# Four layers of graph attention on one core: moved copies, and two groups of VectorE work tied to a place in its order

## The chip, the cores and the metric

The kernel runs on one NeuronCore of one Trainium2 chip. The metric is the device time of one execution in microseconds (us), and smaller is better. A core has TensorE (matmuls), VectorE, ScalarE, GpSimd (POOL) and SyncE (SP), which here only issues transfers. Each engine works through its own list of instructions in order. In profile lines the engines are called PE (its weight loads PEld), DVE, ACT, POOL and SP.

## The reference

Input x is 4096 rows of 256 floats, `adj` a symmetric 4096 x 4096 matrix of zeros and ones with a filled diagonal. Four attention layers follow each other; each adds its result to x and normalises the rows:

```python
x = _layernorm(x + _L0_gnn_ref(x, adj, L0_gnn_W, L0_gnn_a), axis=-1)
x = _layernorm(x + _L1_gnn_ref(x, adj, L1_gnn_Wq, L1_gnn_bq, L1_gnn_Wk, L1_gnn_bk, L1_gnn_Wv, L1_gnn_bv), axis=-1)
x = _layernorm(x + _L2_gnn_ref(x, adj, L2_gnn_W, L2_gnn_a), axis=-1)
x = _layernorm(x + _L3_gnn_ref(x, adj, L3_gnn_Wq, L3_gnn_Wk), axis=-1)
```

The first layer has four heads and additive scores: `e = leaky_relu(s_i + s_j)` with both terms from `h @ W`, masked by `adj`, a softmax over j, the weighted sum of `h @ W`, and an elu. The second has four heads with q, k and v from x, and exponentials of q.k where `adj` has an edge. The third is additive with one head. The fourth takes the cosine between projections of x, its exponential where there is an edge, and returns half of the weighted mean of x plus half of x:

```python
raw_att = Kn @ Qn.T
att = jax.nn.softmax(jnp.where(adj > 0, raw_att, NEG) * TEMP, axis=1)
prop_fea = att @ features
return (1.0 - KEEP_RATIO) * prop_fea + KEEP_RATIO * features
```

## The kernel before, in words

x lies in SBUF for the whole kernel, as tile X of 32 row tiles of 128. The result is made in 8 blocks (NB) of 512 columns (QW); for each block a loop runs over the 32 row tiles j (64 half tiles in the second layer). Such a pair (block, j) is a unit. In each unit ScalarE makes the raw weights, VectorE masks them by a slice of `adj`, and TensorE multiplies them with the features and sums over j in PSUM. TensorE's sums run LAG units behind the weights.

The order on each engine comes from a scheduler, which places instructions by its own idea of their times, except inside a `manual_schedule` block, where the named engines keep the program's order. In the first layer and in the opening of the second this is TensorE alone, in the last layer none until its ending. `tc.issue_after(i)` around an instruction forbids the scheduler to place it ahead of instruction i.

**Start of the first layer** (additive_heads). `turn(b)` transposes block b of x on TensorE (L117) and copies it out of PSUM into xT (L119); `busy` (L357) says on which engines, one copy for each half of the features. `prepare(b)` multiplies it by the weights (L215) into a PSUM tile `side` of three banks and one further bank, takes exponentials (L219 to L221) and stores the values V (L222). For block 0, `first_rows` (L267) lays the source terms of the four heads out as rows in four PSUM banks: one bank of its own for head 0, three of tile `over` for heads 1 to 3. It does so by four transposes a head (L272). `weights(0, 0)` reads these rows straight out of PSUM (L299), one activation a head, and then `keep_rows` (L275) copies them to SBUF, for odd heads on VectorE and for even ones on ScalarE (L277), for later units to read. The mask product is L302, the sums are L312. `first_rows`, `turn(1)`, unit 0, `turn(2)` and `prepare(1)` come in this order, then unit 1.

**Opening of the second layer** (multi_head_attention). Blocks 2 to 7 of x are transposed by `block_apart`: VectorE transposes 32 x 32 squares (L129, two instructions) into a tile of which one buffer exists, SP sends it to DRAM (`far<-squares`, L133) and fetches it back rearranged (`xT<-far`, four transfers, L137). For each block `keys` makes q and k (L755), ScalarE adds the bias (L763), VectorE takes the greatest absolute value of each (L764, into kbig and qbig). `values` makes v (L774) and VectorE stores it (L781). In turn b the program has block_apart(b + 1), values(b - 1), keys(b); the last turn has no values ahead of keys. Before them the first layer's tail for the last block runs (outputs, L324 to L331, add_elu, layernorm), and its `turn(1)` (L747) copies on ScalarE.

**Last layer** (cosine_attention). In each unit `scores` (L1138) and an exponential (L1142) are made; in every second unit `weights` masks two tiles at once (L1151) and `mix_weights` makes three differences (L443 to L445), with which seven products (L453) do the work of eight. After a block `outputs` puts the quarters together and `squares_far` transposes them by squares (L1172), sends them to DRAM (L1176) and fetches them back (L1179) into `kept2`. `outputs_far(b - 1)` is called at j = 10 of the lagging loop of the next block: it sums the fetched rows (L1186), scales and adds them to y (L1190), takes row statistics (one_row, L156 and L157), a root (Ln and Exp on ScalarE, L161 and L162) and stores the rows (L1203).

Of the kernel before, what the change touches and what calls it, by code (L numbers as in the profile page):

```python
# [18 lines left out]
P = 128  # L19
D = 256  # L20
# [8 lines left out]
def kernel(  # L29
# [205 lines left out]
    def additive_heads(a, H, slope, early, narrow, ahead):  # L235
# [7 lines left out]
        with ExitStack() as lay:  # L243
# [23 lines left out]
            def first_rows(banks):  # L267

                row[0] = rp.tile([P, H, QW], FP, name="row")
                for h in range(H):  # L270
                    for k in range(QB):
                        nc.tensor.transpose(banks[h][:, k * P:(k + 1) * P],  # L272
                                            src[:, k, h:h + 1].to_broadcast([P, P]), ident)

            def keep_rows(banks):  # L275
                for h in range(H):
                    (nc.vector.tensor_copy if h % 2 else nc.scalar.copy)(row[0][:, h, :], banks[h])  # L277

            def rows(b, pr):

# [10 lines left out]
            def weights(b, j, rows=None):  # L291
                m = b, j // MJ
                if j % MJ == 0:
                    mask[m] = mp.tile([P, MJ, QW], I32, name="mask")
                    nc.sync.dma_start(mask[m], edges[:, j:j + MJ, b * QW:(b + 1) * QW])
                z = prob[b, j] = zp.tile([P, H, QW], FP, name="prob")
                for h in range(H):
                    r = rows[h] if rows else row[b][:, h, :]
                    nc.scalar.activation(z[:, h, :], r, AF.Relu, bias=-1.0, scale=dst[:, j, h:h + 1])  # L299
                if rows:  # L300
                    keep_rows(rows)
                nc.vector.scalar_tensor_tensor(z, z, 1.0, mask[m][:, j % MJ, :].unsqueeze(1).to_broadcast([P, H, QW]),  # L302
                                               OP.add, OP.mult)

# [49 lines left out]
            def turn(b, bank=bank):  # L354
                if b + 2 < NB:
                    load_x(b + 2)
                busy = (nc.scalar.copy if b == 0 else nc.vector.tensor_copy,  # L357
                        nc.vector.tensor_copy if b == 1 else nc.scalar.copy)
                xTs[b] = transposed_block(sb, bank, b, busy)

            def prepare(b):
# [6 lines left out]
            with tc.manual_schedule(engines={mybir.EngineType.PE}):  # L368


                over = pa.tile([P, HC + 1, QW], FP, name="acc")
                side = pa.tile([P, HC + 1, QW], FP, name="acc")

                def warm(n):

                    for _ in range(n):
                        nc.tensor.matmul(over[:, 0, :P], ones, ones, start=True, stop=True)

                warm(2)
                nc.tensor.matmul(side[:, 0, :], ones[:1, :], a_row, start=True, stop=True)  # L380
                attach(keep, w_sb, side[:, 0, :], H)
                turn(0)
                warm(2)
                prepare(0)
                banks = [bank()] + [over[:, h, :] for h in range(H - 1)]
                first_rows(banks)
                free = iter([side[:, 0, :], side[:, 1, :]])
                turn(1, lambda: next(free))
                for i in range(len(units) + LAG):
                    if i < len(units):  # L390
                        b, j = units[i]
                        weights(b, j, None if i else banks)
                        if (b, j) == (1, 4 * QB):
                            early()
                        if i % 8 == 4:
                            narrow(prob[b, j][:, 0, :1])
                    if i >= LAG:
                        b, j = units[i - LAG]
                        sums(b, j)
                        if b:  # L400
                            finish(b - 1, j)

                    if i == 0 or i % QB == 3 and 3 + i // QB <= NB:
                        b = 1 if i == 0 else 2 + i // QB
                        if b + 1 < NB:
                            turn(b + 1)
                        prepare(b)
                        if b == 3:
                            rows(1, bank())
                    if i == (NB - 1) * NT + 20:  # L410
                        ahead(bank)
# [299 lines left out]
    def multi_head_attention(w_sb, b_sb, tail, rows_of_den, rows_done, narrow_edges, ga):  # L711
# [12 lines left out]
        with ExitStack() as lay:  # L724
# [7 lines left out]
            with ExitStack() as pro:  # L732
# [17 lines left out]
                def keys(b):  # L750
                    for n, to, scale in (("k", kT, 1.0), ("q", qT, qscale)):
                        for o in range(KC):
# [6 lines left out]
                            if n == "q" and b > 1:  # L759
# [1 line left out]
                                part, pk = (t.rearrange(how, a=QB, n=P // QB) for t, how in  # L761
                                            ((part, "p (k a n) -> p a k n"), (pk, "p (a k n) -> p a k n")))
                            nc.scalar.activation(part, pk, AF.Identity, bias=b_sb[n][:, o:o + 1], scale=scale)  # L763
                            nc.vector.tensor_reduce(big[n][:, b, o:o + 1], to[:, o, b * QW:(b + 1) * QW], AX.X, OP.max,  # L764
                                                    apply_absolute_value=True)

                def values(b):

# [35 lines left out]
                with tc.manual_schedule(engines={mybir.EngineType.PE}):  # L804
                    keys(0)
                    tail(bank, own)
                    turn(1)
                    for b in range(1, NB):
                        if b < NB - 1:
                            xTs[b + 1] = block_apart(sb, sq, dr, b + 1, nc.sync)  # L810
                        if b < NB - 1:
                            values(b - 1)
                        keys(b)
                        if b == 2:
                            ga.spread(bank, w2_sb)
                    values(NB - 2)
# [295 lines left out]
    def cosine_attention(co, tail):  # L1112
# [4 lines left out]
        with ExitStack() as lay:  # L1117
# [8 lines left out]
            pa = pool(lay, "co_pa", 1, space=PSUM)  # L1126
            ps = pool(lay, "co_ps", 2, space=PSUM)
            ov = out.rearrange("(t p) d -> p t d", p=P)
            mixed, acc, prob, mix, y, back = {}, {}, {}, {}, {}, {}

            def bank():
                return ps.tile([P, QW], FP, name="g")
# [11 lines left out]
            def weights(b, g):  # L1144
# [6 lines left out]
                nc.vector.tensor_tensor(z, z, co.mask[b, 2 * g // MJ][:, lo:lo + 2, :], OP.mult)  # L1151
                if b < NB - 1 or g < NP - LAST:
                    s = mix[b, g] = sb.tile([P, 4, HW], FP, name="mix")
                    mix_weights(s, z, nc.vector)

            def one_product(b, g, n):
                product(acc[b], prob[b, g], mix[b, g], mixed[g // 2][:, g % 2], g, n)
# [21 lines left out]
                nc.sync.dma_start(t, away.rearrange("r a m q s -> a r (m q s)"))  # L1179
                back[b, h] = t.rearrange("p (k f) -> p k f", k=2)  # L1180

            def outputs_far(b):
                mv = fin.tile([P, QB, 2], FP, name="mv")
                rden = fin.tile([P, QB], FP, name="rden4")
                for h in range(2):
                    nc.vector.tensor_reduce(rden[:, 2 * h:2 * h + 2], back[b, h], AX.X, OP.add)  # L1186
                nc.vector.tensor_scalar_mul(rden, rden, 2.0 / D)
                nc.vector.reciprocal(rden, rden)
                for k in range(QB):
                    nc.vector.scalar_tensor_tensor(y[b][:, k, :], back[b, k // 2][:, k % 2, :], rden[:, k:k + 1], y[b][:, k, :],  # L1190
                                                   OP.mult, OP.add)
                    one_row(mv, k, y[b][:, k, :])
                normalise([y[b][:, k, :] for k in range(QB)], mv)
                store(b, 0, QB, nc.sync)

            def rest(b, k, po, rden, mv):
                nc.vector.scalar_tensor_tensor(y[b][:, k, :], po, rden, y[b][:, k, :], OP.mult, OP.add)
# [88 lines left out]
                store(b, 3, 1, nc.sync)  # L1286

            units = [(b, j) for b in range(NB) for j in range(NT)]
            LAG = 4
            steps = {(0, j + n): (NB - 2 + b, step) for b, j in enumerate((1, 12)) for n, step in ((0, 3), (4, 3), (5, 1), (7, 2), (8, 3))}  # L1290
            for i in range(len(units) + LAG):
                if i < len(units):
                    b, j = units[i]
                    seen = scores(b, j)
                    if j % 2:
                        weights(b, j // 2)
                    if (b, j) == (0, 3):
                        tail(bank, cp)
                    if (b, j) == (0, 0):
# [4 lines left out]
                if i >= LAG:  # L1304
# [7 lines left out]
                    if i - LAG < len(units) - 2 * LAST:  # L1312
                        for n in range(7)[:4] if j % 2 == 0 else range(7)[4:]:
                            one_product(b, j // 2, n)
                        if j == NT - 1:
                            outputs(b)
                    if b and j == 10:
                        outputs_far(b - 1)
            with tc.manual_schedule(engines={mybir.EngineType.PE, mybir.EngineType.DVE, mybir.EngineType.Activation}):
                ending(NB - 1)  # L1320

# [89 lines left out]
```

## Time and profile before

| | us |
|---|---|
| Three runs | 2788.82, 2796.16, 2797.37 |
| Their median | 2796.16 |
| The profiled execution | 2794.14 |
| Its span, first to last instruction | 2792.4 |
| PE busy | 2772.5 |
| DVE busy | 2290.4 |
| ACT busy | 1702.9 |
| POOL busy | 1082.3 |
| The largest group, PE L312, 6144 records | 664.0 |

A group's line gives the kernel's line, the engine, the operation, the written tile, `<-`, the read tiles, and their sizes. In a list in order of time the first number is the start from the span's beginning and the second the stretch that `xN` such instructions took together. `[1.15 <-DVE prob L302]` says that the engine was idle for 1.15 us before it and that VectorE's instruction of line 302 ended this. In a list of waits the numbers are the total in us, how often, and the longest. A matmul of 32-bit floats leaves two records (a transpose one). Matmuls overlap and their ends are modelled, so the records' starts tell more than their ends.

### The profile page before, as it was taken

To read this page: it belongs to the slowest core of one execution; us is meant where nothing else is said; L and a number is where in the kernel's file an instruction comes from. 1 tells how busy PE (TensorE), PEld (TensorE's weight loads), DVE (VectorE), ACT (ScalarE), POOL (GpSimd) and SP (SyncE) were. 2 spreads that over 40 slices of the span, in tenths; PEclk is the share of its full clock that TensorE was granted. 3 is DMA by queue.
4 is the path that set the end of the run, shared out by engine and by line. 5 is a ranking of instruction groups with operands and counts; after the bars stand their busy time and mean duration, and the time that the engine had idled before them with its cause. 6 is when DMAs were issued, how large, how long until landed. Compare 5 with 4: busy or idle time off the path is not lost. (4 is left out here: it accounts for less than half of the span.)

```text
span 2792.4 us, 50485 instructions
## 1 busy us (share of the span) xinstructions
PE 2772.5 (99%) x19557; PEld 1449.7 (52%) x19557; DVE 2290.4 (82%) x3049; ACT 1702.9 (61%) x2668; POOL 1082.3 (39%) x1020
## 2 busy tenths in 40 slices
PE   9999999999999999999999999999999999999999
PEld 5333333333453333333333335888888777776776
DVE  8899999999677788887888878888888877776776
ACT  8899999999336666666666666465556422222222
POOL 0000100100029878778788787455455000000000
PEclk9999999999999999999999999999999999999999
DMA  7566676765339899998988988567778554444442
GB/s 207 107 142 137 138 144 130 136 143 114 69 97 193 184 178 196 192 188 184 195 182 189 190 182 187 174 199 213 181 207 238 109 82 76 77 72 78 72 74 43
DMA packets 275066, 411.94 MB, mean 148 GB/s; under 512 B 54809, under 2 KB 155657, under 8 KB 273930
## 3 DMA queue, kind: packets, MB, share of 16 engines
q0 software_dynamic: 104176, 182.74, 41.4%
q1 hardware_dynamic: 164280, 218.88, 26.2%
q10 hardware_dynamic: 6370, 7.10, 0.8%
q8 instruction: 153, 2.51, 0.4%
q14 instruction: 87, 0.71, 0.1%
HBM read 335.94 MB, written 39.40 MB: 134 GB/s over the span
## 5 line engine op out<-in xcount | busy, mean ns | idle before, releaser
L854 DVE TENSOR_TENSOR prob<-p,mask 128x1024 f32<-128x1024 f32 x512 | 619.7, 1222 | 165.9 <-ACT p L844 159.6
L844 ACT ACTIVATE p<-p,shift 128x1024 f32<-128x1024 f32 x512 | 555.7, 1088 | 319.4 <-PE p L842 319.2
L312 PE MATMUL acc<-prob,V 128*32 128x512 f32 x6144 | 664.0, 592 | 1.2 <-DVE prob L302 1.2
L299 ACT ACTIVATE prob<-row,dst 128x512 f32<-128x512 f32 x1020 | 635.1, 714 | 0.6
L302 DVE SCALAR_TENSOR_TENSOR prob<-prob,mask 128x2048 f32<-128x2048 f32 x256 | 580.4, 2286 | 25.7 <-ACT prob L299 25.0
L864 POOL TENSOR_TENSOR den<-den,prob 128x1024 f32<-128x1024 f32 x220 | 558.5, 2539 | 92.5 <-DVE prob L854 87.2
L842 PE MATMUL p<-qT,kT 64*64 64x512 f32 x4096 | 531.1, 590 | 2.2 <-DVE prob L854 2.2
L878 PE MATMUL acc<-prob,V 64*64 64x512 f32 x4096 | 529.9, 589 | 0.0
L312 PEld LDWEIGHTS acc<-prob,V 128*32 128x32 f32 x6144 | 197.3, 110 | 453.0 <-issue 432.2
L453 PE MATMUL acc<-mix,mixed 128*128 128x256 f32 x1476 | 402.1, 381 | 4.8 <-DVE mix L444 2.9
L453 PEld LDWEIGHTS acc<-mix,mixed 128*128 128x128 f32 x1476 | 278.7, 190 | 49.4 <-DVE mix L444 4.1
L878 PEld LDWEIGHTS acc<-prob,V 64*64 64x64 f32 x4096 | 157.4, 133 | 282.1 <-issue 280.3
L842 PEld LDWEIGHTS p<-qT,kT 64*64 64x64 f32 x4096 | 154.3, 133 | 279.2 <-issue 254.5
L90 POOL COPY tick<-prob 128x1 f32<-128x1 f32 x35 | 38.0, 1086 | 642.8 <-DVE prob L302 641.9
L1151 DVE TENSOR_TENSOR prob<-prob,mask 128x1024 f32<-128x1024 f32 x128 | 156.1, 1219 | 141.6 <-ACT prob L1142 141.6
L870 POOL DMA_DIRECT2D den<-prob x240 | 230.9, 962 | 61.2 <-DMA den<-prob 24.6
L1070 POOL DMA_DIRECT2D mask<-in_adjT x64 | 47.7, 745 | 532.6 <-DVE prob L1151 436.9
L453 PE MATMUL acc<-prob,X 128*128 128x256 f32 x984 | 252.6, 379 | 0.0
L453 PEld LDWEIGHTS acc<-prob,X 128*128 128x128 f32 x984 | 186.7, 190 | 78.8 <-issue 57.1
L586 DVE SCALAR_TENSOR_TENSOR prob<-r,own,mask 128x512 f32<-128x512 f32 x252 | 177.0, 743 | 49.0 <-POOL mix L445 13.0
L1142 ACT ACTIVATE prob<-p 128x512 f32<-128x512 f32 x144 | 86.0, 597 | 202.8 <-PE p L1138 202.8
L1142 ACT ACTIVATE prob<-g 128x512 f32<-128x512 f32 x112 | 66.9, 597 | 208.4 <-PE g L1138 208.4
(239 smaller groups left out, 2849.5 us busy)
## 6 DMA issues: line engine op xcount, KB each, us to landing
mask<-in_adjT SPq DMA_DIRECT2D x254, 512.0 KB
den<-prob POOLq DMA_DIRECT2D x240, 512.0 KB, 5.3
mask<-edges SPq DMA_DIRECT2D x512, 64.0 KB
mask<-in_adjT POOLq DMA_DIRECT2D x64, 512.0 KB, 5.7
edges<-in_adj POOLq DMA_DIRECT2D x32, 512.0 KB, 9.7
far<-squares SPq DMA_DIRECT2D x16, 512.0 KB
den<-prob SPq DMA_DIRECT2D x16, 512.0 KB
row<-far SPq DMA_DIRECT2D x7, 1024.0 KB
```

What stands on the lines that cost most here:

```text
L299: nc.scalar.activation(z[:, h, :], r, AF.Relu, bias=-1.0, scale=dst[:, j, h:h + 1])
L302: nc.vector.scalar_tensor_tensor(z, z, 1.0, mask[m][:, j % MJ, :].unsqueeze(1).to_broadcast([P, H, QW]), OP.add, OP.mult)
L312: nc.tensor.matmul(acc[b][h * G:(h + 1) * G, n, :], part, prob[b, j][:, h, :], start=(j == 0), stop=(j == NT - 1))
L453: nc.tensor.matmul(acc[at][:, half * HW:(half + 1) * HW], w, a, start=(g == 0 and n in (0, 2, 3, 5)), stop=(g == NP - 1), skip_group_check ...
L586: nc.vector.scalar_tensor_tensor(z[:, n, :], r, ga.own[:, j:j + 1], mask[:, n, :], OP.add, OP.mult)
L842: nc.tensor.matmul(p[c * d:(c + 1) * d, r, :], kT[half, c, at:at + d], qT[half, c, cols], start=True, stop=True)
L844: nc.scalar.activation(p, p, AF.Exp, bias=shift)
L854: nc.vector.tensor_tensor(z, p, mask[m][:, j % MJ, :].unsqueeze(1).to_broadcast([P, KC, QW]), OP.mult)
L864: nc.gpsimd.tensor_tensor(to, to, flat, OP.add)
L870: nc.gpsimd.dma_start(to, flat, accum_op=OP.add)
L878: nc.tensor.matmul(acc[b][c][r * d:(r + 1) * d, :], V[half, j, r * d:(r + 1) * d], prob[b, j][half, r, :], start=(j == 0), stop=(j == NH - 1))
L1151: nc.vector.tensor_tensor(z, z, co.mask[b, 2 * g // MJ][:, lo:lo + 2, :], OP.mult)
```

## The change

It has five pieces.

1. `first_rows` itself copies each head's row to SBUF, on VectorE, right after its four transposes; `keep_rows` is gone.
2. `turn(1)` copies both halves on ScalarE, where before VectorE copied both. `turn(2)` and later ones copy the first half on VectorE and the second on ScalarE, as before.
3. `prepare(1)` with its `turn(2)` comes after the weights of unit 1 instead of unit 0.
4. In the second layer's opening `keys` returns its last greatest-value instruction, and the next turn's `block_apart` may not be issued before it.
5. In the last layer `outputs_far` is cut into six steps, called at j = 15, 17, 19, 21, 23 and 25, each tied behind the last difference that `mix_weights` has made by then.

```diff
--- before.py
+++ after.py
@@ -271,10 +271,7 @@
                     for k in range(QB):
                         nc.tensor.transpose(banks[h][:, k * P:(k + 1) * P],
                                             src[:, k, h:h + 1].to_broadcast([P, P]), ident)
-
-            def keep_rows(banks):
-                for h in range(H):
-                    (nc.vector.tensor_copy if h % 2 else nc.scalar.copy)(row[0][:, h, :], banks[h])
+                    nc.vector.tensor_copy(row[0][:, h, :], banks[h])
 
             def rows(b, pr):
 
@@ -297,8 +294,6 @@
                 for h in range(H):
                     r = rows[h] if rows else row[b][:, h, :]
                     nc.scalar.activation(z[:, h, :], r, AF.Relu, bias=-1.0, scale=dst[:, j, h:h + 1])
-                if rows:
-                    keep_rows(rows)
                 nc.vector.scalar_tensor_tensor(z, z, 1.0, mask[m][:, j % MJ, :].unsqueeze(1).to_broadcast([P, H, QW]),
                                                OP.add, OP.mult)
 
@@ -354,8 +349,7 @@
             def turn(b, bank=bank):
                 if b + 2 < NB:
                     load_x(b + 2)
-                busy = (nc.scalar.copy if b == 0 else nc.vector.tensor_copy,
-                        nc.vector.tensor_copy if b == 1 else nc.scalar.copy)
+                busy = (nc.scalar.copy if b < 2 else nc.vector.tensor_copy, nc.scalar.copy)
                 xTs[b] = transposed_block(sb, bank, b, busy)
 
             def prepare(b):
@@ -400,8 +394,8 @@
                         if b:
                             finish(b - 1, j)
 
-                    if i == 0 or i % QB == 3 and 3 + i // QB <= NB:
-                        b = 1 if i == 0 else 2 + i // QB
+                    if i == 1 or i % QB == 3 and 3 + i // QB <= NB:
+                        b = 1 if i == 1 else 2 + i // QB
                         if b + 1 < NB:
                             turn(b + 1)
                         prepare(b)
@@ -761,8 +755,9 @@
                                 part, pk = (t.rearrange(how, a=QB, n=P // QB) for t, how in
                                             ((part, "p (k a n) -> p a k n"), (pk, "p (a k n) -> p a k n")))
                             nc.scalar.activation(part, pk, AF.Identity, bias=b_sb[n][:, o:o + 1], scale=scale)
-                            nc.vector.tensor_reduce(big[n][:, b, o:o + 1], to[:, o, b * QW:(b + 1) * QW], AX.X, OP.max,
-                                                    apply_absolute_value=True)
+                            last = nc.vector.tensor_reduce(big[n][:, b, o:o + 1], to[:, o, b * QW:(b + 1) * QW], AX.X,
+                                                           OP.max, apply_absolute_value=True)
+                    return last
 
                 def values(b):
 
@@ -805,12 +800,14 @@
                     keys(0)
                     tail(bank, own)
                     turn(1)
+                    last = None
                     for b in range(1, NB):
                         if b < NB - 1:
-                            xTs[b + 1] = block_apart(sb, sq, dr, b + 1, nc.sync)
+                            with tc.issue_after(getattr(last, "ins", last)) if last is not None else nullcontext():
+                                xTs[b + 1] = block_apart(sb, sq, dr, b + 1, nc.sync)
                         if b < NB - 1:
                             values(b - 1)
-                        keys(b)
+                        last = keys(b)
                         if b == 2:
                             ga.spread(bank, w2_sb)
                     values(NB - 2)
@@ -1126,7 +1123,7 @@
             pa = pool(lay, "co_pa", 1, space=PSUM)
             ps = pool(lay, "co_ps", 2, space=PSUM)
             ov = out.rearrange("(t p) d -> p t d", p=P)
-            mixed, acc, prob, mix, y, back = {}, {}, {}, {}, {}, {}
+            mixed, acc, prob, mix, y, back, norm = {}, {}, {}, {}, {}, {}, {}
 
             def bank():
                 return ps.tile([P, QW], FP, name="g")
@@ -1151,7 +1148,7 @@
                 nc.vector.tensor_tensor(z, z, co.mask[b, 2 * g // MJ][:, lo:lo + 2, :], OP.mult)
                 if b < NB - 1 or g < NP - LAST:
                     s = mix[b, g] = sb.tile([P, 4, HW], FP, name="mix")
-                    mix_weights(s, z, nc.vector)
+                    return mix_weights(s, z, nc.vector)
 
             def one_product(b, g, n):
                 product(acc[b], prob[b, g], mix[b, g], mixed[g // 2][:, g % 2], g, n)
@@ -1179,19 +1176,32 @@
                 nc.sync.dma_start(t, away.rearrange("r a m q s -> a r (m q s)"))
                 back[b, h] = t.rearrange("p (k f) -> p k f", k=2)
 
-            def outputs_far(b):
-                mv = fin.tile([P, QB, 2], FP, name="mv")
-                rden = fin.tile([P, QB], FP, name="rden4")
-                for h in range(2):
-                    nc.vector.tensor_reduce(rden[:, 2 * h:2 * h + 2], back[b, h], AX.X, OP.add)
-                nc.vector.tensor_scalar_mul(rden, rden, 2.0 / D)
-                nc.vector.reciprocal(rden, rden)
-                for k in range(QB):
-                    nc.vector.scalar_tensor_tensor(y[b][:, k, :], back[b, k // 2][:, k % 2, :], rden[:, k:k + 1], y[b][:, k, :],
-                                                   OP.mult, OP.add)
-                    one_row(mv, k, y[b][:, k, :])
-                normalise([y[b][:, k, :] for k in range(QB)], mv)
-                store(b, 0, QB, nc.sync)
+            def outputs_far(b, step, seen):
+
+                with tc.issue_after(getattr(seen, "ins", seen)):
+                    if step == 0:
+                        rden = fin.tile([P, QB], FP, name="rden4")
+                        for h in range(2):
+                            nc.vector.tensor_reduce(rden[:, 2 * h:2 * h + 2], back[b, h], AX.X, OP.add)
+                        nc.vector.tensor_scalar_mul(rden, rden, 2.0 / D)
+                        nc.vector.reciprocal(rden, rden)
+                        norm[b] = rden, fin.tile([P, QB, 2], FP, name="mv")
+                    elif step < 3:
+                        rden, mv = norm[b]
+                        for k in (2 * step - 2, 2 * step - 1):
+                            nc.vector.scalar_tensor_tensor(y[b][:, k, :], back[b, k // 2][:, k % 2, :], rden[:, k:k + 1],
+                                                           y[b][:, k, :], OP.mult, OP.add)
+                            one_row(mv, k, y[b][:, k, :])
+                    elif step == 3:
+                        norm[b] += begin_root(norm[b][1])
+                    else:
+                        _, mv, v, r, n = norm[b]
+                        if step == 4:
+                            end_root(v, r, n)
+                        for k in (2 * step - 8, 2 * step - 7):
+                            scale_row(y[b][:, k, :], mv, r, k)
+                        if step == 5:
+                            store(b, 0, QB, nc.sync)
 
             def rest(b, k, po, rden, mv):
                 nc.vector.scalar_tensor_tensor(y[b][:, k, :], po, rden, y[b][:, k, :], OP.mult, OP.add)
@@ -1286,14 +1296,14 @@
                 store(b, 3, 1, nc.sync)
 
             units = [(b, j) for b in range(NB) for j in range(NT)]
-            LAG = 4
+            LAG, mixes = 4, None
             steps = {(0, j + n): (NB - 2 + b, step) for b, j in enumerate((1, 12)) for n, step in ((0, 3), (4, 3), (5, 1), (7, 2), (8, 3))}
             for i in range(len(units) + LAG):
                 if i < len(units):
                     b, j = units[i]
                     seen = scores(b, j)
                     if j % 2:
-                        weights(b, j // 2)
+                        mixes = weights(b, j // 2) or mixes
                     if (b, j) == (0, 3):
                         tail(bank, cp)
                     if (b, j) == (0, 0):
@@ -1314,8 +1324,8 @@
                             one_product(b, j // 2, n)
                         if j == NT - 1:
                             outputs(b)
-                    if b and j == 10:
-                        outputs_far(b - 1)
+                    if b and j in (15, 17, 19, 21, 23, 25):
+                        outputs_far(b - 1, (j - 15) // 2, mixes)
             with tc.manual_schedule(engines={mybir.EngineType.PE, mybir.EngineType.DVE, mybir.EngineType.Activation}):
                 ending(NB - 1)
```

## The prediction, made before the changed kernel ran

> **What bounds the kernel now.** I read the busy times first, then what TensorE waited for, then the stretch around each wait in order of time.
>
> ```profile
> PE 2772.5 (99%) x19557; PEld 1449.7 (52%) x19557; DVE 2290.4 (82%) x3049; ACT 1702.9 (61%) x2668; POOL 1082.3 (39%) x1020
> ```
>
> TensorE is idle for 2792.4 - 2772.5 = 19.9 us in all. The change neither adds nor removes a matmul, and in the built programs TensorE's instructions stand in the same order before and after. So it can only win back waits, or add some.
>
> ```profile
> PE acc L453 <- DVE mix L444: 2.9, 1, 2.9
> ...
> PE g L755 <- ACT xT L119: 1.2, 1, 1.2
> PE acc L312 <- DVE prob L302: 1.2, 1, 1.2
> ...
> PE acc L215 <- DVE xT L119: 0.5, 1, 0.5
> PE pv L774 <- DVE V L781: 0.3, 1, 0.3
> ```
>
> In TensorE's waits (total us, times, longest) these five lie where the diff reaches. The first is in the last layer:
>
> ```profile
> 2581.00 0.69 DVE L1186 TENSOR_REDUCE rden<-kept 128x2 f32<-128x512 f32 x1 [6.95 <-DMA kept<-away]
> 2581.60 0.42 DVE L444 TENSOR_TENSOR mix<-prob,mix 128x256 f32<-128x256 f32 x1
> ...
> 2582.07 1.27 PE L453 MATMUL acc<-mix,mixed 128*128 128x256 f32 x4 [2.88 <-DVE mix L444]
> ...
> 2583.14 1.91 PE L1138 MATMUL g<-T,T 128*128 128x512 f32 x2
> ```
>
> VectorE stood 6.95 us in front of a fetched row, with the mixing L444 queued behind it, and TensorE ran dry for 2.88 us. The next scores took 1.91 us for two, where they take 1.02 elsewhere. Busy times by stretch (PE busy, PEld, DVE, ACT, POOL, then granted clock, DMA share, GB/s) say why:
>
> ```profile
> 2579.00:2582.00 3.00, 0.19 (x1) 0.00 (x0) 1.00 (x3) 0.00 (x0) 0.00 (x0) 1.00 0.21 47
> 2583.20:2586.60 3.40, 3.40 (x8) 2.07 (x7) 3.40 (x9) 0.60 (x1) 0.00 (x0) 0.54 0.00 0
> ```
>
> After the idle stretch the clock fell to 0.54 for 3.4 us, which costs about half of that, 1.7. The other two places, first the opening of the second layer and then the kernel's start:
>
> ```profile
> 733.02 1.30 DVE L129 STREAM_TRANSPOSE squares<-X 128x512 f32<-128x512 f32 x2 [6.09 <-DMA far<-squares]
> ...
> 737.80 3.70 PE L755 MATMUL g<-xT,wk_sb 128*128 128x512 f32 x8 [1.19 <-ACT xT L119]
> ```
>
> ```profile
> 12.04 0.75 PE L272 MATMUL g<-ident,src 128*128 128x128 f32 x4
> 12.63 1.47 PE L272 MATMUL acc<-ident,src 128*128 128x128 f32 x12
> ...
> 16.35 2.94 PE L215 MATMUL acc<-w_sb,xT 128*128 128x264 f32 x12 [0.51 <-DVE xT L119]
> ...
> 16.51 0.69 DVE L277 COPY row<-acc 128x512 f32<-128x512 f32 x1 [0.21 <-ACT prob L299]
> ...
> 20.11 2.78 PE L312 MATMUL acc<-prob,V 128*32 128x512 f32 x24
> ...
> 24.05 2.78 PE L312 MATMUL acc<-prob,V 128*32 128x512 f32 x24 [1.15 <-DVE prob L302]
> ```
>
> **What the Trainium skill says.** "TensorE: Matmul & The Clock Gate", under HAM oscillation, warns of idle gaps over about 3.4 us, after which the clock is halved. The trace agrees in kind; here 2.88 us was enough. The same page (Architectural detail) calls ScalarE and VectorE strict first-in first-out, as L444 behind L1186 shows. "PSUM — Partial Sum Buffer", under PSUM bank collisions, wants two engines kept apart by bank, two readers too. The trace has it: VectorE's copy at 16.51 waits for a ScalarE read. "DMA: Bandwidth & Descriptors", under Anatomy of one DMA, puts about 2 us of fixed cost on each transfer (fitted for another queue than SP's). Here far<-squares, issued at 780.17, let xT<-far issue at 782.87, 2.7 us later.
>
> **Part C, outputs_far in six steps behind the mixings.** Before, the second reduce stands 16 us behind the last squares transpose (end 2557.95, would have begun at 2574.05). Landing took up to 23.0 us (2581.00). In the after program it stands behind the eighth group's mixing: the second group's mask began at 2562.63, groups come every 4.74 us, so the eighth begins at 2591.07 and is mixed 2.75 later, 2593.8. That is 36 us after the squares against 23.0, so the fetch wait goes, and so do 2.9 + 1.7 = 4.6 us. Another block's reduce at 2273.9 idled 4.05 us with no TensorE wait listed: about 4 us is free, and beyond that it counts in full. Each step adds to one group: two updates, two statistics and two aggregates come to about 2 x (0.44 + 0.37 + 0.1) = 1.8 us, hidden in VectorE's 1.9 us wait for ScalarE per group. If that cover were gone, a step would cost up to 1.8 us less some 3.5 us by which mixing runs ahead (mixing ends 2570.8, its product starts 2574.3), so nothing. ScalarE's two root instructions (0.2 us each) wait for VectorE at about 2.9 us after the group's last exponential; the exponential queued behind them is due at about 4.1. The store on SP waits for step five, at unit 30; the next block's SP transfers start three units (7 us) after the block's end, so nothing is held. POOL's order is unchanged. Both ends: a gain of 4.6 (observed) down to 0.
>
> **Part B, squares bound behind the last reduce.** The double at 733.02 was early work of block 3; the one squares buffer made it wait 6.09 us, and the previous layer's tail, queued behind it, came late (neg at 736.54). In the after order that transpose stands behind the last reduce of block 1. The tail's reciprocal can start when its TensorE product is there, about 731.2, so the tail moves up some 4 us, ScalarE's xT copies follow the transposes (end 733.16), and keys(1) follows values(0) at 736.6 instead of 737.80. I take back 1.35 (start to start beyond the matmuls' pace at 737.8) plus 0.26 and 0.48 at 745.1 and 747.35, where values had not been evacuated: 2.1 us. What is late next: squares now start after keys(b-1). From squares' end to xT landed I read 6.2 us (780.14 to 786.36, DMA records) and 8.3 in the slow case (766.87 to 775.2). Matmuls between are 10.5 us for blocks 3 to 6, since block pitch is 10.32, and about 7.4 for block 7, which has no values ahead of its keys. So 0 is lost at 6.2 and 0.9 at 8.3. SP's order changes only in that block 3's far issue moves behind block 2's four xT issues. Value: -2.1, ends -2.5 and -1.0.
>
> **Part A, first rows on VectorE.** This is where I expect a loss. first_rows now interleaves four transposes and a copy per head. In the after program the third head's transposes wait for VectorE's copy of the second, and the fourth's for the third's, although their banks differ: the dependence is kept by tile. Before, no such wait exists. Walking it with the durations above (PSUM copy 0.69, ScalarE 0.69 at a pitch of 0.62, four transposes 0.6): copies at 12.92 and 13.54; third head 14.27 to 14.87; copy to 15.60; fourth head 15.64 to 16.24; copy to 16.97. The next eight transposes end at 17.12 instead of 14.98. ScalarE, which has put five later activations first, copies xT[1] from 17.42 to 18.6, so L215 starts at 18.63, not 16.35. Unit 0's last three activations end at 20.46, its mask product at 22.78; its sums start at 22.82 (20.11 before), unit 1's follow without a wait at 25.39 (24.05 before). So the two waits of 0.5 and 1.15 go, but larger ones come: +1.3 us net, and TensorE, saturated from 31 us on, never gives it back. Moving prepare(1) behind weights(1) changes no TensorE order and costs 0. Ends: 0 (copies overlap better), and +3.0 if the thin stretch from 13.2 to 18.6 lowers the clock once (+1.7).
>
> **Sum.** Against the profiled execution's own 2794.14 (span 2792.4 and 1.7 around it): -4.6 - 2.1 + 1.3 = -5.4, 2788.7. The runs shown are 2788.82, 2796.16 and 2797.37. I read the spread as zero to two such stalls of 4.6, since the stall-free profile would be 2789.5. From the lowest run: 2788.82 - 2.1 + 1.3 = 2788.0. I take 2788.2 for all executions, since the varying part is gone; against the median of 2796.16 that is -8.0, -0.28%.
>
> **Rivals.** 0.3% is 8.4 us, about what a measurement of this kernel can tell from no change: the line is at 2787.8.
> - *Main case*, 58%: 2785.7 to 2790.5. Its centre is 2788.2 and about half of it is below the line.
> - *Lower floor*, 27%: the lowest run too held a stall, or the start costs nothing; 2784 to 2787.8. For: one profiled execution has one stall, so a run with none may be rare. Against: 2789.5 fits 2788.82 well.
> - *It doesn't do what it says*, 10%: a fetch longer than 36 + 4 us, or the clock lost at the start, leaves 2 to 6 us: 2790.5 to 2795.
> - *Slower*, 5%: the opening's round trip at L129, L133, L137 becomes the bound. For b = 3 to 7 the cost is 4 x (R - 10.6) + (R - 7.4). It costs from 8.3 us on only in the last block, and needs R = 13.2 us, twice the usual, to give 16.4 us and pass 2804.6. Against: five records of it (blocks 3 to 7) lie at 6.2 to 8.3.
>
> Faster: half of 58 plus 27 = 0.56; within: 29 + 10 = 0.39; slower 0.05. The range 2785.0 to 2792.5 leaves out the slower case, half of the third and the lowest piece of the second, some 16%.
>
> **What would show it.** In the changed profile: no wait of VectorE for kept<-away, full clock through the last layer, squares waits near 0 and keys(1) following values(0) without a gap; at the start, gaps between the four heads' transposes and the first L312 sums near 22.8. I'm wrong if those sums start before 20.1, if keys(7) waits for xT, or if TensorE waits for mix in every block.

## The result and the profile after

The changed kernel takes **2788.14 us** (median of 22 runs, 2785.07 to 2789.70); the kernel before, run beside it, 2790.52 (22 runs, 2788.21 to 2797.37). The medians differ by 2.4 us. The ratio, which is reckoned from all runs and not from the medians (their quotient is 0.9991), is 0.9987, 95% interval 0.9982 to 0.9993: a small gain that is clear of zero and within the 0.3% named above. The profiled execution took 2789.70 with a span of 2787.9 (before 2794.14 and 2792.4).

The busy times of the page, after:

```profile
PE 2771.8 (99%) x19557; PEld 1450.8 (52%) x19557; DVE 2300.1 (83%) x3049; ACT 1703.8 (61%) x2668; POOL 1086.2 (39%) x1020
```

TensorE is idle for 2787.9 - 2771.8 = 16.1 us, 3.8 less than before. Its waits (total us, times, longest):

```profile
PE p L839 <- DVE prob L851: 2.1, 3, 1.0
PE acc L272 <- DVE row L274: 1.8, 2, 1.0
...
PE acc L371 <- DVE ones L73: 1.1, 1, 1.1
PE acc L447 <- DVE quarters L469: 1.0, 5, 0.2
```

The five waits shown of before (on mix, xT twice, prob in the first sums, V) are gone. One is new, on the first rows: this is part A. The start, in order of time:

```profile
12.27 0.75 PE L272 MATMUL g<-ident,src 128*128 128x128 f32 x4
12.85 0.60 PE L272 MATMUL acc<-ident,src 128*128 128x128 f32 x4
...
14.48 0.65 PE L272 MATMUL acc<-ident,src 128*128 128x128 f32 x4 [1.03 <-DVE row L274]
...
15.91 0.65 PE L272 MATMUL acc<-ident,src 128*128 128x128 f32 x4 [0.79 <-DVE row L274]
16.40 1.62 PE L117 MATMUL acc<-ident,X 128*128 128x128 f32 x8
...
19.52 3.13 PE L215 MATMUL acc<-w_sb,xT 128*128 128x264 f32 x12
...
23.47 5.36 PE L307 MATMUL acc<-prob,V 128*32 128x512 f32 x48
...
28.76 1.09 PE L117 MATMUL g<-ident,X 128*128 128x128 f32 x8
```

The third and fourth head's transposes wait 1.03 and 0.79 us for VectorE's copies. Eight transposes of X take 1.62 us where they took 1.04. The busy times by stretch (columns as in the prediction) name the reason:

```profile
12.00:16.40 4.40, 2.59 (x18) 1.81 (x18) 3.12 (x5) 2.84 (x8) 0.00 (x0) 1.00 1.07 371
16.40:19.80 3.40, 3.40 (x19) 3.40 (x18) 1.38 (x2) 2.94 (x6) 0.00 (x0) 0.54 1.07 363
```

The clock was halved for one step of 3.41 us, from 16.70 on. From the first head's transposes to the first ones behind the second sums is 28.76 - 12.27 = 16.49 us; before it was 26.76 - 12.04 = 14.72.

The opening of the second layer, part B:

```profile
726.80 0.70 DVE L129 STREAM_TRANSPOSE squares<-X 128x512 f32<-128x512 f32 x1
...
733.34 0.18 DVE L324 RECIPROCAL rden<-g 128x4 f32<-128x4 f32 x1 [0.64 <-PE g L319]
...
735.00 3.62 PE L769 MATMUL pv<-wv_sb,xT 128*128 128x256 f32 x16
...
738.45 3.60 PE L749 MATMUL g<-xT,wk_sb 128*128 128x512 f32 x8
```

No 6.09 us wait for the squares buffer stands here. The tail's reciprocal runs as soon as its product is there, and keys(1) follows values(0) without a gap. The last layer, part C:

```profile
2593.87 0.43 DVE L439 TENSOR_TENSOR mix<-prob,mix 128x256 f32<-128x256 f32 x1
2594.22 1.27 DVE L1185 TENSOR_REDUCE rden<-kept 128x2 f32<-128x512 f32 x2
2596.16 1.22 DVE L1148 TENSOR_TENSOR prob<-prob,mask 128x1024 f32<-128x1024 f32 x1 [0.26 <-ACT prob L1139]
```

Both reduces run behind the eighth group's mixing with no wait for kept<-away. The clock, which before fell at 2582.94, stays full here:

```profile
2583.20:2586.60 3.40, 3.40 (x15) 2.56 (x14) 1.54 (x3) 1.14 (x2) 0.74 (x1) 1.00 0.45 51
```

### The profile page after: what moved, and what is told of

Read it like the earlier page. It is cut to its first block, busy times and chain, and to the rows that moved or that the text cites. A ratio compares the mean times of both kernels' runs of the same rounds, so it can differ in the third digit from the quotient of the medians.

```text
span 2787.9 us, 50482 instructions
## 1 busy us (share of the span) xinstructions
PE 2771.8 (99%) x19557; PEld 1450.8 (52%) x19557; DVE 2300.1 (83%) x3049; ACT 1703.8 (61%) x2668; POOL 1086.2 (39%) x1020
```

## The experiments

Twelve kernels ran, e5 being the kernel before once more, in three groups of four (e1 to e4, e5 to e8, e9 to e12), each group on another chip and beside runs of the kernel before there (medians 2791.52, 2791.20 and 2791.57). I call these runs the neighbours. The median of e5 lies 1.3 us above that of its neighbours, which are the same kernel, so a difference of about 1 us between medians decides nothing by itself. Beside the times I read three sizes from every trace. *Start*: from the first head's transposes to the transposes of X behind the second sums. *Opening* and *last layer*: by how much TensorE's start times fall behind the pace of its own matmuls between 700 and 800 us, and between 2200 and 2700 us.

| Kernel | parts | median us (runs) | ratio to before, 95% | start | opening | last layer |
|---|---|---|---|---|---|---|
| before, profiled | none | see above | 1 | 14.72 | 2.78 | 5.26 |
| changed | A B C | 2788.14 (22) | 0.9987 [0.9982, 0.9993] | 16.49 | 0.44 | 0.00 |
| e1 | B C | 2786.82 (19) | 0.9980 [0.9973, 0.9987] | 14.72 | 0.44 | 0.00 |
| e2 | A | 2792.30 (14) | 0.9997 [0.9989, 1.0006] | 16.48 | 2.33 | 2.27 |
| e3 | B | 2788.31 (22) | 0.9986 [0.9979, 0.9992] | 14.72 | 0.43 | 2.04 |
| e4 | C | 2789.57 (22) | 0.9990 [0.9983, 0.9996] | 14.72 | 2.79 | 0.00 |
| e5 | none | 2792.46 (13) | 1.0007 [0.9999, 1.0015] | 14.73 | 2.72 | 2.42 |
| e6 | A, copies behind; B C | 2785.12 (12) | 0.9977 [0.9968, 0.9985] | 13.88 | 0.44 | 0.00 |
| e7 | A B; C in one piece | 2788.33 (21) | 0.9987 [0.9981, 0.9994] | 15.72 | 0.44 | 0.00 |
| e8 | A B; C early | 2788.02 (21) | 0.9985 [0.9978, 0.9992] | 15.72 | 0.44 | 0.00 |
| e9 | two squares buffers | 2793.75 (21) | 1.0006 [1.0000, 1.0013] | 14.72 | 5.08 | 1.46 |
| e10 | A B | 2788.56 (13) | 0.9991 [0.9983, 0.9999] | 16.49 | 0.44 | 1.06 |
| e11 | reduces behind a mixing | 2788.30 (21) | 0.9989 [0.9982, 0.9996] | 14.71 | 3.08 | 0.00 |
| e12 | A, other banks; B C | 2786.27 (15) | 0.9981 [0.9973, 0.9988] | 15.21 | 0.43 | 0.00 |

### One part at a time

**e1**: the first layer as before, the other parts kept.

```
-                    nc.vector.tensor_copy(row[0][:, h, :], banks[h])
+            def keep_rows(banks):
+                for h in range(H):
+                    (nc.vector.tensor_copy if h % 2 else nc.scalar.copy)(row[0][:, h, :], banks[h])
...
-                    if i == 1 or i % QB == 3 and 3 + i // QB <= NB:
+                    if i == 0 or i % QB == 3 and 3 + i // QB <= NB:
```

> The changed kernel with the first rows put back as they were (part A undone; B and C kept). My theory: A costs 2.0 us, read from the first sums at 23.47 instead of 20.11 us and the transposes after the second group at 28.76 instead of 26.76. So this one is 2.0 below the changed kernel, 2786.1, and its clock stays full from 10 us on. Rival, the start is made up before the end: equal to the changed kernel, 2788.1.

2786.82: 1.3 below the changed kernel, or 2.3 when each is taken against its own neighbours (4.7 and 2.4 below them). So A does cost, and it isn't made up; how much of the expected 2.0, the times can't tell. The start gives 1.77: some 0.2 of my 2.0 was the later moment at which the changed kernel's execution came to the first heads (12.27 against 12.04), and not A.

**e2**: the same lines the other way, in the kernel before.

> The kernel before with part A alone. My theory: +2.0 on the median of 2790.5, so 2792.5, with the gaps of about 1.0 and 0.8 us ahead of the third and fourth head's transposes and one stretch of about 3.4 us at half clock near 16.5 us. Rival, A is free: 2790.5.

2792.30, a median 0.8 above its neighbours' with a ratio just below 1; the interval holds 1, so the times show no cost here. Both gaps (1.03 and 0.78 us) and the clock's fall, at 16.40 us, are in its trace, and its start is 16.48.

**e3**: the kernel before with the squares bound.

```
...
-                            xTs[b + 1] = block_apart(sb, sq, dr, b + 1, nc.sync)
+                            with tc.issue_after(getattr(last, "ins", last)) if last is not None else nullcontext():
+                                xTs[b + 1] = block_apart(sb, sq, dr, b + 1, nc.sync)
...
-                        keys(b)
+                        last = keys(b)
```

> The kernel before with part B alone (the transposes into squares bound behind the last reduce). My theory: -2.1, so 2788.4, and the wait of 6.09 us at the opening of the second layer is gone. Rival, the 2 us are absorbed later, since VectorE's waits further on take them: 2790.5.

2788.31, next to the expected 2788.4, which was reckoned from 2790.52; against its own neighbours the gain is 3.2, a good 1 more than the wait explains. The opening falls from 2.78 to 0.43.

**e4**: the kernel before with outputs_far in six steps.

> The kernel before with part C alone (outputs_far in six bound steps). My theory: no wait for a fetched row in the last layer and a flat delay of TensorE there. The stall of 4.6 us that it removes comes in some executions only, so the slowest runs go (none above 2792) and the median falls by about 2.2 to 2788.3, while the lowest stays near 2788. Rival 1, the profiled execution of before was an exception and C is worth nothing in the median: 2790.5. Rival 2, C is worth the whole 4.6 in every run: 2786.

2789.57: 1.95 below its neighbours, near my 2.2 and between the two rivals. The last layer is flat, and one run (2793.87) lies above the 2792 that I had set as the highest.

**e5**: the kernel before, unchanged.

> The kernel before, unchanged, as a control. Of its 86 executions so far 17 lie above 2795, while none of the 36 of the two kernels that keep outputs_far as it was but have part A or part B alone does, which the stall in the last layer does not explain. If the tail is a property of this kernel, about 4 of 22 lie above 2795 and the median is near 2791.5. Rival, the tail belongs to when a kernel runs in its round: none of 22, and a median near 2790.

2792.46, with 3 of 13 above 2795: the tail is the kernel's own. This execution shows what the last layer of before costs when no fetch is as late as the one that the prediction found at 2581.00. That one ran 23.1 us behind its squares, the latest here 21.4. VectorE's waits for the fetch, then TensorE's for the mixing:

```profile
DVE rden L1186 <- DMA kept<-away: 11.8, 5, 5.3
```

```profile
PE acc L453 <- DVE mix L444: 1.4, 2, 1.2
```

The prediction's reading that about 4 us of such a wait are free and the rest counts in full holds here too: 5.3 us left TensorE 1.2 us idle, and in e2 4.8 us left it 0.7.

### Part A: the engine or the order

**e6**: the same four VectorE copies, behind all sixteen transposes.

```
                     for k in range(QB):
                         nc.tensor.transpose(banks[h][:, k * P:(k + 1) * P],
                                             src[:, k, h:h + 1].to_broadcast([P, P]), ident)
-                    nc.vector.tensor_copy(row[0][:, h, :], banks[h])
+                for h in range(H):
+                    nc.vector.tensor_copy(row[0][:, h, :], banks[h])
```

> The changed kernel with the four VectorE copies written behind all sixteen transposes instead of between the heads. My theory: A's cost is not the move to VectorE but the heads' waits, kept by tile, and the clock that falls in them. Here no transpose waits, the clock stays full, xT is copied at about 16.4 us, the first sums start near 20.9 and the second follow without a wait, so the transposes after them come about 0.5 us earlier than in the kernel before: 2.3 below the changed kernel, 2785.8. Rival, VectorE's four serial copies are the cost: no better than the changed kernel, 2788.1.

2785.12: 3.0 below the changed kernel, and 6.1 below its neighbours, where the changed kernel is 2.4 below its own. Its start:

```profile
11.26 0.75 PE L272 MATMUL g<-ident,src 128*128 128x128 f32 x4
11.84 1.47 PE L272 MATMUL acc<-ident,src 128*128 128x128 f32 x12
...
13.15 1.04 PE L117 MATMUL acc<-ident,X 128*128 128x128 f32 x8
13.36 1.89 DVE L275 COPY row<-acc 128x512 f32<-128x512 f32 x3 [0.54 <-PE acc L272]
...
19.86 5.36 PE L308 MATMUL acc<-prob,V 128*32 128x512 f32 x48 [0.25 <-DVE prob L298]
...
25.14 1.09 PE L117 MATMUL g<-ident,X 128*128 128x128 f32 x8
```

No transpose waits, the clock stays full, and the start is 13.88: 0.84 less than in the kernel before, 2.61 less than in the changed one. So writing the copies between the heads is what costs, 2.61 at the start; with the copies behind the transposes part A gains 0.84. Of its three pieces (copies on VectorE, `turn(1)` on ScalarE, the later `prepare(1)`) no run moves one alone, so which of them gains isn't shown.

**e12**: the changed kernel with a bank of another tile between the first two.

```
-                banks = [bank()] + [over[:, h, :] for h in range(H - 1)]
+                banks = [over[:, 0, :], bank()] + [over[:, h, :] for h in range(1, H - 1)]
```

> The changed kernel with the heads' banks in another order: head 0 in the tile that holds three banks, head 1 in a tile of its own, heads 2 and 3 in the first tile again. My theory: the wait follows the tile and not the engine, so head 2 now waits for the copy of head 0, which is done about 0.7 us sooner: its wait falls from 1.03 to 0.3 or less, while head 3 still waits some 0.8 for head 2's copy. 0.7 less than the changed kernel, 2787.4, or more if the clock no longer falls. Rival, every head waits for the copy ahead of it whatever its tile: 2788.1 with both waits as before.

2786.27 (2787.4 expected). The third head waits less, since the last copy from its tile is one earlier; the fourth as before:

```profile
12.39 0.68 DVE L274 COPY row<-acc 128x512 f32<-128x512 f32 x1
...
12.99 0.68 DVE L274 COPY row<-g 128x512 f32<-128x512 f32 x1
13.13 0.65 PE L272 MATMUL acc<-ident,src 128*128 128x128 f32 x4 [0.43 <-DVE row L274]
...
14.57 0.65 PE L272 MATMUL acc<-ident,src 128*128 128x128 f32 x4 [0.79 <-DVE row L274]
```

The third head starts when the first head's copy, from its own tile but another bank, is done (13.07), while the second head's copy from the other tile still runs (until 13.67). The wait follows the tile, not the bank and not the copy just ahead. The clock stays full here.

### Part C: the place or the cut

**e7**: all six steps at once, behind the eighth group's mixing.

```
-                    if b and j in (15, 17, 19, 21, 23, 25):
-                        outputs_far(b - 1, (j - 15) // 2, mixes)
+                    if b and j == 15:
+                        for step in range(6):
+                            outputs_far(b - 1, step, mixes)
```

> The changed kernel with outputs_far in one piece behind the eighth group's mixing. My theory: it is the later place that takes the fetch wait away. The piece is about 7 us of VectorE work (1.5 for the reduces and reciprocals, 3.6 for updates and statistics, some 2 for the root and scaling) against about 4 to 5 us that are free per group, so at most a few tenths per block come back: 2788.1 to 2790. Rival, the cut into six is what helps: TensorE waits for mix in each of seven blocks, 2 us or more each, above 2800.

2788.33 and the last layer flat: no gain of the cut into six is to be seen.

**e8**: the six steps four groups earlier, `j in (7, 9, 11, 13, 15, 17)`.

> The changed kernel with the six steps four groups earlier (19 us), about 17 us behind the squares, where a fetched row was seen to land 16 to 23 us behind them. My theory: VectorE waits for kept<-away again in most blocks, up to 7 us in one; what passes about 4.5 us shows as a TensorE wait for mix. Median 2789 to 2790, with some executions several us above it. Rival, the cut and not the place helps: 2788.1 with a spread like the changed kernel's.

The waits for the fetch come back, in three of seven blocks, but none reaches TensorE: 2788.02, and no run above 2789.26. My theory falls: the early place costs nothing that these runs show.

```profile
2572.33 0.42 DVE L439 TENSOR_TENSOR mix<-prob,mix 128x256 f32<-128x256 f32 x1
2572.67 0.68 DVE L1185 TENSOR_REDUCE rden<-kept 128x2 f32<-128x512 f32 x1
2576.58 0.69 DVE L1185 TENSOR_REDUCE rden<-kept 128x2 f32<-128x512 f32 x1 [3.23 <-DMA kept<-away]
2577.60 1.21 DVE L1148 TENSOR_TENSOR prob<-prob,mask 128x1024 f32<-128x1024 f32 x1
```

Two things differ from the kernel before. There the second reduce is due 16.1 us behind the last squares transpose, between two instructions of a mixing; here it is due at 17.6 us, behind a whole mixing. The longest wait is 3.2 us, inside the 4 that were seen to be free even in the middle of a mixing, so the 1.5 us may be enough; no run parts the two.

**e11**: the kernel before, outputs_far whole and at j = 10, bound behind the last mixing put out before it.

```
...
                     if b and j == 10:
-                        outputs_far(b - 1)
+                        with tc.issue_after(getattr(mixes, "ins", mixes)):
+                            outputs_far(b - 1)
```

> The kernel before with outputs_far whole and at its old place in the program, but bound behind the last mixing put out before it, so that its reduces stand between two groups and about one group (4.7 us) later, not inside a mixing. My theory after the early steps cost nothing: this one bound is enough, since a wait between groups has the lead of about 3.5 us by which mixing runs ahead plus the group's slack before TensorE runs dry. 2789.6 as with part C alone, no run above 2794. Rival, only the eighth group or the six steps are late or small enough: 2791 to 2792 with the tail.

2788.30, no slower than C alone, no run above 2790.17, the last layer flat.

```profile
2579.58 0.43 DVE L445 TENSOR_TENSOR mix<-prob,mix 128x256 f32<-128x256 f32 x1
2579.93 1.27 DVE L1186 TENSOR_REDUCE rden<-kept 128x2 f32<-128x512 f32 x2
```

The second reduce stands 22.3 us behind the squares, 6.2 later than before, and waits in no block. One bound does what the six steps do. Since it comes after the fetch has landed, this run doesn't show what the place behind a mixing is worth for a reduce that has to wait.

**e10**: the changed kernel with outputs_far as before.

> The changed kernel with part C undone (A and B kept). My theory: C is worth 1.5 (changed kernel without A, 2786.8, against B alone, 2788.3) to 2.0 (C alone against before), so 2789.6 to 2790.1, with TensorE waits for mix of about 1 us in all in a typical profile. If the slow tail of before is the last layer's stall and nothing else, about a fifth of the runs lie 4 us or more above the median. Rival, A or B alone has removed that tail, as the runs of each suggest: all runs within 3 us of the median.

2788.56, 0.4 above the changed kernel but 3.0 below its neighbours (the changed kernel 2.4), so in the times C's worth beside A and B doesn't show. All runs lie within 3.2 us of the median: the rival's picture. In its trace the last layer loses 1.06, with waits for the fetch of at most 4.3 us.

### Part B: the buffer or the order

**e9**: the kernel before with two squares buffers, no bound.

```
-                sq = pool(pro, "mh_sq", 1)
+                sq = pool(pro, "mh_sq", 2)
```

> The kernel before with two squares buffers at the opening of the second layer, and no bound. My theory for part B: the wait of 6.09 us is for the one buffer, and the late tail behind it is the cost. With two buffers the transposes of two blocks run early without waiting, keys(1) follows values(0) without a gap, and about the 2.1 to 3.2 of the squares bound alone come back: 2788.3 to 2789.5. Rival, early transposes in front of the tail cost as much as the wait, or the round trip is what TensorE waited for: 2791.

2793.75, a median 2.2 above its neighbours', the interval just touching 1: no gain, and a cost above the rival's 2791. The lines of this kernel:

```profile
724.66 1.89 DVE L129 STREAM_TRANSPOSE squares<-X 128x512 f32<-128x512 f32 x3
...
733.20 1.30 DVE L129 STREAM_TRANSPOSE squares<-X 128x512 f32<-128x512 f32 x2 [6.08 <-DMA far<-squares]
734.99 1.29 DVE L129 STREAM_TRANSPOSE squares<-X 128x512 f32<-128x512 f32 x2
...
736.77 0.17 DVE L329 RECIPROCAL rden<-g 128x4 f32<-128x4 f32 x1
...
739.17 5.40 PE L755 MATMUL g<-xT,wk_sb 128*128 128x512 f32 x8 [2.70 <-ACT xT L119]
```

With room for one block more, the scheduler put two blocks more of squares in front of the tail: block 3 now fits at 724.66 behind the end of block 2, block 4 takes over the wait of 6.08 us, and block 5 stands behind it with another 1.29 us. The reciprocal comes at 736.77 (735.40 before), TensorE waits 2.70 for xT instead of 1.19, and its clock falls (5.40 us for eight matmuls, where the same eight of the second weights took 3.60 at 727.24). So what B gains is the order: no squares that wait ahead of the tail.

## Why the prediction was right, point by point

The time was right to 0.1 us, partly by luck (see the sum), and the signs of all three parts were right. Of the sizes, B's held, A's was close and C's was that of an exception. The gain was much smaller than forecast, 2.4 us and not 8.0, since the 8.0 were reckoned from a median of three runs, 2796.16, where 22 runs gave 2790.52. So the likeliest outcome of the prediction, at 0.56 a gain of more than 0.3%, didn't come.

- **Part A, +1.3.** The walk through the tile's dependence was right: waits at the heads foreseen and found. With the clock kept (e7, e8) the start costs 15.72 - 14.72 = +1.00; with its fall +1.77 (changed kernel, e2, e10). The fall, which I held for an end, came in three of five profiles of this order. Timed, A is +1.3 (e1 to the changed kernel), 2.3 with the neighbours taken off, or +0.8 (e2), too far apart to choose between these sizes. The first sums were to start near 22.8; they came at 23.47. One reading was loose: VectorE's copy at 16.51 starts after the last of ScalarE's three reads of `over`, which ends at 16.48, so this wait may go with the whole tile and doesn't by itself show two readers kept apart by bank.
- **Part B, -2.1.** Four profiles without B and with one buffer besides the profiled one give 2.33 to 3.08 at the opening, all with B 0.43 or 0.44: -2.3, next to -2.1. keys(7) didn't wait for xT. The times give more, -3.2 (e3) and -2.75 from e4 to e1, but the rest is no larger than the 1.3 of e5.
- **Part C, -4.6.** For the profiled execution it was right: 5.26 went. Its weight in the other executions was the mis-sized term. I read "zero to two such stalls of 4.6" from three runs. Five other profiles with outputs_far unbound and at its old place (e2, e3, e5, e9, e10) lose 1.06 to 2.42 in this layer, and the clock doesn't fall in it. So in the usual execution C removes a loss of 1 to 2.4 us and not of zero or 4.6: timed 1.95 (e4), 1.5 (e3 to e1), 0.4 (e10 to the changed kernel). Whether the slowest executions held a large stall is open (below). The lowest run of before, which I took as free of stalls, need not have been.
- **The sum.** With the sizes of a usual execution: +1.0 to +1.8, -2.3, -1.1 to -2.4, so -1.6 to -3.7; measured -2.4 against 2790.52. The starting point, 2788.82 minus 2.1 plus 1.3, hit the time since C's omitted 1 to 2 and a lowest run 1.7 below the median nearly cancel. That is luck.
- **In the profiled pair** the three parts give 1.77 - 2.34 - 5.26 = -5.8; the spans differ by -4.5. Most of the difference is +1.27 between 800 and 2200 us, where the change does nothing and the fourteen profiles lose from 12.35 to 15.03, and 0.23 of a later start.
- **The rivals.** "It doesn't do what it says" fails on the traces, "slower" too: xT's round trip never became the bound. (The prediction's sum for a round trip of 13.2 us gives 16.2 and not 16.4, which changes nothing.) The median stayed above "lower floor", 2784 to 2787.8.

**What stays open.** 35 of 201 runs of the kernel before, and 3 of 13 of the control, lie above 2795. None of the 49 runs of the three kernels does that keep outputs_far as it was and have A, B or both. With C the late fetch has nothing to stop; why A or B alone should keep these executions away, no run tells. The granted clock listed for the runs of the twelve sets says a little more. A mean of 0.998 stands in 18 of them, 16 of before, one of e5 and one of e9, and all 18 lie above 2795; the profiled executions have 0.999 or 1.0, those with one fall 0.999. So in about half of the slow tail the clock was lost for longer than in any profile, which fits stalls like the one that the prediction found; where they lie, no profile shows.

## What to carry to other kernels

Read a stall as a wait plus what stands behind it: a bound that takes the waiting instruction from in front of a late tail (B), or moves it behind the landing that it waits for (e11), does the work, while one more buffer let the scheduler put more in front (e9). Where copies and transposes share one tile, write the copies behind all transposes. Before a stall of one profiled execution is put into a sum for the median, look for it in a second execution.

## What the runs showed of the hardware

- TensorE's clock changed on a grid of 3.41 us that starts where it first rose: in all fourteen traces every later change lies a whole number of such steps behind it. TensorE's idle time within one step, with ends as the profile models them and leaving out each kernel's last microseconds, parts the steps that a fall followed from all others. In the changed kernel the clock rose at 9.87 and fell at 16.70, after a step with gaps of 1.03 and 0.79 us; e2 and e10, with both gaps in one step, fell too, and so did the kernel before (2.55 us in the step) and e9 (2.70). In e7 (rose at 7.14) and e8 (11.25) a step's edge divides the same gaps, at most 1.5 us in one, and the clock held. The most idle time without a fall was 1.59 us, in e11. The Trainium skill ("TensorE: Matmul & The Clock Gate", HAM oscillation) has gaps over about 3.4 us; here 1.8 us in a step was enough, in two pieces, and the measurement decides.
- The first head's transposes start at 11.12 to 13.15 us in these traces, though nothing ahead of them was changed. The two ends are those of the clock's first rise: 7.14 in e7 with 11.12, 11.25 in e8 with 13.15.
- Where outputs_far stood at its old place, unbound, the second reduce ran 16.0 to 21.4 us behind the last squares in all profiles but the first, where one waited until 23.1. In that case the fetch's records (2575.00 to 2580.58) lie beside those of a 512 KB mask load (2575.11 to 2581.22); for the same block of the changed kernel it began 1.3 us ahead of the mask load and took 3.2 us instead of 5.6. That this is the cause was only argued.
